# Differential attention and a routed expert layer on one core: projecting queries and keys for eight heads at once, spreading them by DMA, and a new order of the side work

## The chip, the cores and the metric

The kernel runs on one NeuronCore of a Trainium2 chip. Its engines are TensorE (PE, matrix products), VectorE (DVE), ScalarE (ACT), GpSimd (POOL) and SyncE (SP, which here only issues DMAs). Each works through its own queue of instructions in order; semaphores tie the queues together. The metric is the time on the device, in microseconds, of one execution. Three runs of the kernel before gave 842.52, 847.56 and 846.54 us, median 846.54.

## The reference, cut to what matters

The input x is eight sequences of 256 tokens with 256 features, 2048 tokens in all. Two blocks follow each other, each on a layer-normalized copy, each added to x.

```python
q = (x @ wq.T).reshape(b, t, 16, 2, 8);  k = likewise;  v = (x @ wv.T).reshape(b, t, 16, 16)
attn = attn(q1, k1, v) - lambda_full * attn(q2, k2, v)     # softmax over the 256 tokens of a sequence
attn = attn * rsqrt(mean(attn * attn) + eps) * subln_w * (1 - LAMBDA_INIT)
x = x + attn @ wo.T
logits = xn @ gate_w.T                                      # 32 experts
sel = top 4 of logits;  w = softmax over the chosen four
x = x + sum over sel of w * expert(xn) + 0.05 * sum over sel of w * small_expert[sel // 2](xn)
```

There are 16 heads, each with two queries and two keys of 8 features (the two halves of the head) and values of 16 features. The large experts have an inner size of 96, the sixteen small ones of 128; each is silu(gate) times up, then down. All data are 32-bit floats.

## The kernel before, in words

**Tiling.** The 2048 tokens are taken in four iterations (`NIT`) of 512 tokens (`TB`, two sequences). Four heads make a group, so an iteration has four steps and attention has 16 steps, numbered s. A step's K and Q lie with four heads in four blocks of 32 rows: a head has 16 rows of features (8 of each half), one row that takes the maximum of each half, and unused rows.

**Projection (`project`, L319 to L340).** The weights are copied once into padded tiles `wk_pad` and `wq_pad` (L135 to L140) in which every head has 32 columns, 16 of them zero. One product of 128 padded columns with 512 tokens (L327, two halves of the contraction) gives a step's K, another its Q, already in the four blocks. ACT copies Q to `qT`, and K twice to `kb`, once for each half, with the other half's rows cleared and the row that subtracts the maximum set (`half`, L337).

**A slot (`both`, L345).** A step has eight slots i. In each, PE makes scores (sc, L358) for step s and, for a step that lies `AHEAD` = 4 slots on, the products from which the row maxima come (sm, L375). ACT takes the exponential of sc (L385), DVE the maximum of sm (L388). sc and sm share three large PSUM buffers (`big`); one small one (`one`) serves everything else. `join_max` (mt, L399) turns the eight slots' maxima and adds them to Q. In odd slots `values` (pv, L412) multiplies probabilities by values, two slots late; `normalize` (po, L430) turns the result, DVE divides by the sums and POOL adds the two halves of a head (L442).

**Side work.** `prologue(it)` normalizes an iteration's tokens, transposes them (tp_a) and makes values (vps, L303). `epilogue(it)` squares and scales the attention output, transposes it (tp_o), multiplies with wo (L476), adds x, normalizes again (tp_f) and calls `route`: logits (lg, L498), the top four one after another (L511 to L530, six DVE operations for each), a mask, running counts and a product that gives every token its position in the list of each expert (pos, L546). Sixteen indirect DMAs from POOL (L582) scatter token number and weight into the lists in HBM. Both functions are generators that yield "pe" or "any"; `fill` (L598) lets one "any" piece go at every slot and one "pe" piece at slots 1, 5 and 7. The order on PE, ACT and DVE is what the program writes (`manual_schedule`); POOL's and SP's is set by a scheduler. The epilogue of iteration it starts in the third slot of the next iteration's first step; that of iteration 3 has nothing to run beside.

**After attention.** The lists are read back, and 95 tiles of 128 list entries go through the experts: POOL fetches token rows (L751), PE multiplies (gu L785, dn L809 and L813), POOL adds the results to HBM (L820). Weights of the small experts and the down weights of the large ones (`wr_sb`, L670 to L679) are loaded by SP into room that attention held, so after attention. The gate and up weights of the large experts (`wl_sb`, L120) are loaded at the start.

Of the kernel before, what the change touches and what calls it, by code (L numbers as in the profile page):

```python
# [14 lines left out]
MANUAL = {mybir.EngineType.PE, mybir.EngineType.Activation, mybir.EngineType.DVE}  # L15

P = 128
# [21 lines left out]
def kernel(  # L39
# [23 lines left out]
    keep = ctx.enter_context(tc.tile_pool(name="keep", bufs=3))  # L63
# [31 lines left out]
    wraw = p1.tile([P, 2, 2, E], F32)  # L95
    for i, w in enumerate((wk, wq)):
        nc.scalar.dma_start(out=wraw[:, i], in_=w.rearrange("(kc p) o -> p kc o", p=P))
# [3 lines left out]
    w_sb = {}  # L101
    for n, w in (("v", wv), ("o", wo)):
        w_sb[n] = (p1 if n == "v" else const).tile([P, 2, E], F32, name=f"w{n}_sb")
        nc.scalar.dma_start(out=w_sb[n], in_=w.rearrange("(kc p) o -> p kc o", p=P))
# [6 lines left out]
    load_x(1)  # L111
# [21 lines left out]
    wpad = {}  # L133
    for i, n in enumerate(("k", "q")):
        wpad[n] = p1.tile([P, 2, H, 32], F32, name=f"w{n}_pad")  # L135
        nc.gpsimd.memset(wpad[n], 0.0)
        nc.vector.tensor_copy(
            wpad[n][:, :, :, 0 : 2 * D],
            wraw[:, i].rearrange("p kc (h d) -> p kc h d", d=2 * D),
        )  # L140


# [3 lines left out]
    )  # L146

    nlam = const.tile([P, 1], F32)

    def late_constants():  # L150
# [37 lines left out]
        ebase, [[SLOTS, NE]], base=0, channel_multiplier=0, allow_small_or_imprecise_dtypes=True  # L188
# [34 lines left out]
    with actx:  # L223
# [53 lines left out]
        def transpose_rows(src, dst, tag):  # L277
            for kc in range(2):
                yield "pe"
                tp = one(f"tp_{tag}_{kc}")  # L280
                for a in range(NA):
                    nc.tensor.transpose(
                        tp[:, a * P : (a + 1) * P], src[:, a, kc * P : (kc + 1) * P], ident
                    )
                nc.scalar.copy(dst[:, kc, :], tp)
# [3 lines left out]
        def prologue(it):  # L289
            if it and it + 1 < NIT:  # L290
                load_x(it + 1)
            xT = p2.tile([P, 2, TB], F32, tag="xT", name=f"xT_{it}")
            yield from layernorm_T(x_sb[it], xT, f"a{it}")
            vaug = vaugs[it % 2]
            attn = r2.tile([P, NA, H, 2 * D], F32, tag="attn", name=f"attn_{it}")
            st_it[it] = (xT, vaug, attn)
            for a2 in range(NA // 2):
                yield "pe"
                pv = one(f"vps_{it}_{a2}")
                for i in range(2):  # L300
                    a = 2 * a2 + i
                    for kc in range(2):
                        nc.tensor.matmul(  # L303
                            pv[:, i * E : (i + 1) * E],
                            lhsT=xT[:, kc, a * P : (a + 1) * P],
                            rhs=w_sb["v"][:, kc, :],
                            start=(kc == 0),
                            stop=(kc == 1),
                        )
                nc.scalar.copy(  # L310
                    vaug[:, 2 * a2 : 2 * a2 + 2, :, 0 : 2 * D],
                    pv.rearrange("p (a h d) -> p a h d", a=2, d=2 * D),
                )
# [3 lines left out]
        qT, qa, kb, pv, pts = {}, {}, {}, {}, {}  # L317

        def project(s, w):  # L319


            it, g = steps[s]
            cols = slice(g * 4 * 32, (g + 1) * 4 * 32)
            ps = one(f"{w}ps_{s}")
            wv_ = wpad[w].rearrange("p kc h d -> p kc (h d)")
            for kc in range(2):
                nc.tensor.matmul(  # L327
                    ps, lhsT=wv_[:, kc, cols], rhs=st_it[it][0][:, kc, :],
                    start=(kc == 0), stop=(kc == 1),
                )  # L330
            if w == "q":
                qT[s] = p2.tile([P, TB], F32, tag="qT", name=f"qT_{s}", bufs=3)
                nc.scalar.copy(qT[s], ps)
                return
            kb[s] = p2.tile([P, 2, TB], F32, tag="kb", name=f"kb_{s}", bufs=3)
            for h in range(2):
                nc.scalar.activation(  # L337
                    kb[s][:, h, :], ps, AF.Identity,
                    bias=half[:, 1, h : h + 1], scale=half[:, 0, h : h + 1],
                )  # L340
# [66 lines left out]
        def values(s, c):  # L407
# [11 lines left out]
            if c % 2 == 1:  # L419
                oT = p2.tile([P, 512], F32, tag="oT", name=f"oT_{s}_{c}")  # L420
                nc.scalar.copy(oT, pv[s])
                pv[s] = oT

        def normalize(s, bb, oT):
            it, g = steps[s]
            attn = st_it[it][2]
# [6 lines left out]
            pov = po.rearrange("p (r d) -> p r d", d=32)  # L433
            r = p2.tile([P, 16], F32, tag="rsum", name=f"r_{n}")
            nc.vector.reciprocal(r, pov[:, :, 2 * D])
            nc.vector.tensor_scalar(r[:, 8:16], r[:, 8:16], nlam, None, ALU.mult)
            on = p2.tile([P, 16, 2 * D], F32, tag="on", name=f"on_{n}", bufs=3)
# [3 lines left out]
            )  # L441
            nc.gpsimd.tensor_tensor(  # L442
# [6 lines left out]
        def epilogue(it):  # L449
            attn = st_it.pop(it)[2]  # L450
            av = attn.rearrange("p a h d -> p (a h) d")
            yield "any"
            sq = r1.tile([P, NA * H, 2 * D], F32, tag="sq", name=f"sq_{it}")
            nc.gpsimd.tensor_tensor(sq, av, av, ALU.mult)
            yield "any"
# [8 lines left out]
            nc.vector.tensor_tensor(  # L464
                av, av, rms.unsqueeze(2).to_broadcast([P, NA * H, 2 * D]), ALU.mult
            )
            aT = r2.tile([P, 2, TB], F32, tag="eT", name=f"aT_{it}")
            yield from transpose_rows(attn.rearrange("p a h d -> p a (h d)"), aT, f"o{it}")
            xt = x_sb[it]
            for a2 in range(NA // 2):  # L470
                yield "pe"
                ps = one(f"wo_{it}_{a2}")
                for i in range(2):
                    a = 2 * a2 + i
                    for kc in range(2):
                        nc.tensor.matmul(  # L476
                            ps[:, i * E : (i + 1) * E],
                            lhsT=aT[:, kc, a * P : (a + 1) * P],
                            rhs=w_sb["o"][:, kc, :],
                            start=(kc == 0),  # L480
                            stop=(kc == 1),
                        )
                xs = xt[:, 2 * a2 : 2 * a2 + 2, :]
                nc.vector.tensor_tensor(xs, xs, ps.rearrange("p (a e) -> p a e", a=2), ALU.add)
# [6 lines left out]
        def route(it, x2):  # L491
# [16 lines left out]
            chosen = r1.tile([P, TOPK, NA, NE], F32, tag="chosen", name=f"chosen_{it}")  # L508
            top = r2.tile([P, TOPK, NA], F32, tag="top", name=f"top_{it}")
            left = lg  # L510
            for k in range(TOPK):  # L511
                yield "any"
                nc.vector.tensor_reduce(top[:, k], left, AX.X, ALU.max)

                eq = r2.tile(shape, F32, tag="eq", name=f"eq_{it}_{k}")
                nc.vector.tensor_tensor(
                    eq, left, top[:, k].unsqueeze(2).to_broadcast(shape), ALU.is_equal
                )
                nc.vector.tensor_tensor(eq, eq, rev.unsqueeze(1).to_broadcast(shape), ALU.mult)
                mi = r2.tile([P, NA], F32, tag="mi", name=f"mi_{it}_{k}")  # L520
                nc.vector.tensor_reduce(mi, eq, AX.X, ALU.max)
                nc.vector.tensor_tensor(
                    chosen[:, k], eq, mi.unsqueeze(2).to_broadcast(shape), ALU.is_equal
                )
                if k < TOPK - 1:
                    nxt = r2.tile(shape, F32, tag="left", name=f"left_{it}_{k}")
                    nc.vector.scalar_tensor_tensor(
                        nxt, chosen[:, k], -3.0e38, left, ALU.mult, ALU.add
                    )
                    left = nxt  # L530

            yield "any"
            mask = r1.tile(shape, F32, tag="mask", name=f"mask_{it}")
            nc.vector.tensor_reduce(
                mask, chosen.rearrange("p k a e -> p a e k"), AX.X, ALU.add
            )
            yield "any"
            for a in range(NA):
                n = it * NA + a
                nc.vector.tensor_tensor(count[:, n + 1], count[:, n], mask[:, a], ALU.add)  # L540
            yield "pe"
            pos = one(f"pos_{it}")[:, 0 : NA * NE]
            for i, (w, r) in enumerate(
# [12 lines left out]
            entry = r2.tile([P, TOPK, NA, 2], F32, tag="entry", name=f"entry_{it}")  # L556
            wt = entry[:, :, :, 1]
            w4 = [P, TOPK, NA]
            ex = r2.tile(w4, F32, tag="ex", name=f"ex_{it}")
            nc.vector.tensor_tensor(  # L560
                ex, top, top[:, 0].unsqueeze(1).to_broadcast(w4), ALU.subtract
            )
            nc.scalar.activation(ex, ex, AF.Exp)
# [48 lines left out]
        with tc.manual_schedule(engines=MANUAL):  # L612
# [42 lines left out]
            while side:  # L655
                fill()
# [252 lines left out]
```

## Time and profile before

One execution was profiled. It took 878.54 us, of which the span from first to last instruction is 876.8 us; the unprofiled runs have a median of 846.54 us. Times below are from the profiled execution.

| What | us |
|---|---|
| profiled execution, its span | 878.54, 876.8 |
| first maximum product (sm) starts | 24.19 |
| first scores (sc) start | 41.99 |
| Q projections of steps 3 and 12 start | 79.15, 296.88 |
| last transposes of attention (po) start | 448.73 |
| last list scatter is issued, lists are read | 529.68, 533.99 |
| first expert product starts | 543.06 |
| PE busy | 720.9 (82%) |
| DVE, ACT, POOL busy | 374.0 (43%), 322.8 (37%), 339.6 (39%) |

Two things help in reading it. A busy PE is not PE at its peak, since matmuls are pipelined and their ends are modelled. And the share of an engine over the whole span is an average over stages that have different limits, so each stage is read by itself: which instruction waited, and what ended that wait.

### The profile page before, as it was taken

What the parts mean: (1) busy time and instruction counts of PE and PEld (TensorE: products, weight loads), DVE (VectorE), ACT (ScalarE), POOL (GpSimd) and SP (SyncE); (2) the same over time, 40 slices, a digit from 0 to 9 for tenths busy, and PEclk for the clock granted to TensorE, in tenths of its full rate; (3) what the DMA queues carried; (4) which work ended last, traced back from release to release, by engine and by line L of the source; (5) the groups of instructions that cost most, each with busy time, mean ns of one, the idle gap of its engine ahead of it and who ended that gap; (6) DMA issues with size and microseconds to landing.
All of it is one profiled execution on the core that took longest, in us unless ns stands there. A gap on an engine that the chain in (4) does not pass through costs nothing.

```text
span 876.8 us, 11981 instructions
## 1 busy us (share of the span) xinstructions
PE 720.9 (82%) x4201; PEld 429.9 (49%) x4201; DVE 374.0 (43%) x843; ACT 322.8 (37%) x593; POOL 339.6 (39%) x314
## 2 busy tenths in 40 slices
PE   3899999999999869999465302999999999999930
PEld 1334333444444324344244201899777777777720
DVE  1664557655676535776046500233322222222202
ACT  2155445654655333645241100333333333333310
POOL 3000001000010430103410655588888888888850
PEclk9999999999999969999785555999999999999975
DMA  9900000000100000100049801354555455555557
GB/s 267 282 1 1 1 1 1 1 1 26 49 1 1 2 0 4 46 1 2 1 125 237 166 1 44 58 85 81 84 82 83 83 85 85 84 81 84 83 90 253
DMA packets 60300, 58.34 MB, mean 67 GB/s; under 512 B 23122, under 2 KB 56659, under 8 KB 59731
## 3 DMA queue, kind: packets, MB, share of 16 engines
q0 software_dynamic: 20336, 25.12, 17.9%
q1 hardware_dynamic: 36706, 29.32, 12.4%
q10 hardware_dynamic: 3200, 3.15, 1.2%
q8 instruction: 36, 0.59, 0.3%
q14 instruction: 22, 0.17, 0.1%
HBM read 35.73 MB, written 21.82 MB: 66 GB/s over the span
## 4 chain that ended last, share of the span: by engine, by line
PE 68%; DVE 12%; DMA 9%; issue 3%; another core or an unknown queue 3%; POOL 3%; ACT 2%; POOLq 0%; SPq 0%; DVEq 0%; ACTq 0%
PE gu L785 18%; PE sm L375 9%; DVE mp L388 8%; PE sc L358 7%; PE pv L412 6%; PE dn L809 4%; PE dn L813 4%; PE kps L327 4%; PE qps L327 4%; PE xt L759 3%; DMA list_dram<-entry,index 3%; POOL list_dram L582 2%; PE wo L476 2%; DMA y<-sums 2%
## 5 line engine op out<-in xcount | busy, mean ns | idle before, releaser
L388 DVE TENSOR_REDUCE mp<-sm 128x4 f32<-128x1024 f32 x128 | 156.1, 1223 | 145.7 <-PE sm L375 132.1
L385 ACT ACTIVATE pt<-sc 128x1024 f32<-128x1024 f32 x128 | 130.7, 1022 | 144.8 <-PE sm L375 113.7
L820 POOL DMA_INDIRECT sums<-ye,tokens x95 | 151.3, 1593 | 38.7 <-issue 25.0
L358 PE MATMUL sc<-qa,kb 32*128 32x256 f32 x1024 | 163.7, 420 | 2.0 <-issue 1.3
L442 POOL TENSOR_TENSOR attn<-on 128x128 f32<-128x128 f32 x32 | 16.9, 529 | 369.3 <-DVE on L438 354.8
L375 PE MATMUL sm<-kb,qT 32*128 32x512 f32 x512 | 141.1, 650 | 16.6 <-DVE mp L388 9.0
L761 DVE COPY xTe<-xt 128x256 f32<-128x256 f32 x95 | 40.3, 425 | 211.6 <-PE xt L759 199.6
L358 PEld LDWEIGHTS sc<-qa,kb 32*128 32x128 f32 x1024 | 81.8, 187 | 57.0 <-issue 41.9
L751 POOL DMA_INDIRECT xg<-x_dram,tokens x95 | 93.2, 981 | 32.2 <-PE gu L785 13.7
L785 PE MATMUL gu<-wr_sb,xTe 128*128 x380 | 99.3, 384 | 0.0
L785 PE MATMUL gu<-wl_sb,xTe 128*128 x380 | 86.0, 349 | 8.1 <-issue 5.4
L582 POOL DMA_INDIRECT list_dram<-entry,index x64 | 62.2, 972 | 66.4 <-DVE entry L578 39.3
L785 PEld LDWEIGHTS gu<-wl_sb,xTe 128*128 128x128 f32 x380 | 62.2, 192 | 35.9 <-DVE aTe L802 30.2
L785 PEld LDWEIGHTS gu<-wr_sb,xTe 128*128 128x128 f32 x380 | 70.8, 193 | 5.2
L412 PE MATMUL pv<-pt,vaug 128*32 128x512 f32 x512 | 69.9, 619 | 0.1
L794 ACT ACTIVATE act<-gu 128x224 f32<-128x224 f32 x95 | 33.9, 357 | 80.3 <-PE gu L785 70.9
L375 PEld LDWEIGHTS sm<-kb,qT 32*128 32x128 f32 x512 | 37.4, 185 | 47.8 <-DVE mp L388 33.9
L819 ACT ACTIVATE ye<-dn,weights 128x256 f32<-128x256 f32 x95 | 44.8, 472 | 36.8 <-DMA sums<-ye,tokens 32.5
L803 ACT ACTIVATE aTe<-at 128x128 f32<-128x128 f32 x95 | 26.3, 277 | 84.4 <-DVE aTe L802 75.9
L809 PE MATMUL dn<-wr_sb,aTe 96*128 x190 | 56.7, 380 | 0.0
L813 PE MATMUL dn<-wr_sb,aTe 128*128 x190 | 56.6, 379 | 0.0
L759 PE MATMUL xt<-ident,xg 128*128 128x128 f32 x190 | 38.3, 284 | 4.0 <-DMA xg<-x_dram,tokens 3.8
(162 smaller groups left out, 772.0 us busy)
## 6 DMA issues: line engine op xcount, KB each, us to landing
wl_sb<-in_wg_dram SPq DMA_DIRECT2D x4, 768.0 KB, 8.2
wl_sb<-in_wu_dram SPq DMA_DIRECT2D x4, 768.0 KB, 7.4
wr_sb<-in_wd_dram SPq DMA_DIRECT2D x2, 1536.0 KB, 20.8
x<-in_x_dram SPq DMA_DIRECT2D x4, 512.0 KB, 4.2
sums<-zero SPq DMA_DIRECT2D x8, 256.0 KB, 3.2
sums<-x SPq DMA_DIRECT2D x4, 512.0 KB, 2.9
x_dram<-xn_f SPq DMA_DIRECT2D x4, 512.0 KB, 4.4
wr_sb<-in_cwg_dram SPq DMA_DIRECT2D x2, 1024.0 KB, 11.1
```

Source lines behind the costliest of these rows:

```text
L327: nc.tensor.matmul(ps, lhsT=wv_[:, kc, cols], rhs=st_it[it][0][:, kc, :], start=(kc == 0), stop=(kc == 1),)
L358: nc.tensor.matmul(sc[:, j, h * 256 : h * 256 + 256], lhsT=kb[s][rows, h, c * P : (c + 1) * P], rhs=qa[s][rows, qs], start=True, stop=True,)
L375: nc.tensor.matmul(sm[:, j, :], lhsT=qT[m][rows, a * P : (a + 1) * P], rhs=kb[m][rows, :, ks], start=True, stop=True,)
L385: nc.scalar.activation(pt, sc, AF.Exp, scale=SM_SCALE)
L388: nc.vector.tensor_reduce(mps[m % 2][:, a, 2 * mp : 2 * mp + 2, 2 * D : 2 * D + 2], sm.rearrange("p j (s k) -> p j s k", s=2), AX.X, ALU.max,)
L412: nc.tensor.matmul(pv[s][32 * j : 32 * j + 32, :], lhsT=st_it[it][1][:, c, 4 * g + j, :], rhs=pts[(s, c, j // 2)][:, j % 2, :], start=(c % ...
L582: put = nc.gpsimd.indirect_dma_start(list_dram, bass.IndirectOffsetOnAxis(ap=index[:, k, a : a + 1], axis=0), entry[:, k, a], None,)
L751: nc.gpsimd.indirect_dma_start(xg[i], None, x2_dram, bass.IndirectOffsetOnAxis(ap=tokens[:, i : i + 1], axis=0),)
L785: nc.tensor.matmul(ps[:, :, cols], lhsT=xT[i][:, kc, :], rhs=w[:, bass.ds(at + kc * n, n)], start=(kc == 0), stop=(kc == 1),)
L809: nc.tensor.matmul(ps, lhsT=aT[i][0:INTER, 0], rhs=wr[0:INTER, bass.ds(large, E)], start=True, stop=False,)
L813: nc.tensor.matmul(ps, lhsT=aT[i][:, 1], rhs=wr[:, bass.ds(small + (2 * E + 2 * GS), E)], start=False, stop=True,)
L820: nc.gpsimd.indirect_dma_start(sums_dram[i % 2], bass.IndirectOffsetOnAxis(ap=tokens[:, i : i + 1], axis=0), y, None, compute_op=ALU.add, ...
```

## The change: what it does

- K and Q are projected from the unpadded weights: one product gives 128 features, which is eight heads or two steps. It is cut into two parts of 256 tokens. ACT copies the result to a packed tile, and `spread` moves rows by DMA on SP into four standing Q tiles (four DMAs of 16 rows a step) and four standing K tiles (eight DMAs of 8 rows a step). POOL presets these tiles once at the start, so that the rows no DMA writes hold zeros or the row for the maximum.
- SP joins the engines whose order the program writes. All four loads of x are issued at the start, ahead of the gate and expert weights.
- `AHEAD` is 3. Projections sit in slots 0 and 2 of even steps (Q) and 4 and 6 of odd ones (K); po and mt move to slots 3, 5 and 7. Side pieces for PE go into the slots that are left. The pieces are larger: both halves of a transposition, all of vps and all of wo go in one, in a `big` buffer.
- The product with the lambda goes from DVE to POOL, as do the square and the scaling of the epilogue, except in the last iteration.
- The top four come from DVE's operation that returns the eight largest values of a row, with a second one on a key that settles ties, and a third one that finds the four slots. The weights are then picked by comparison.
- A list scatter is a piece of its own ("put"), one for each slot of the program.
- The last epilogue has three `big` buffers to itself.

```diff
-MANUAL = {mybir.EngineType.PE, mybir.EngineType.Activation, mybir.EngineType.DVE}
+MANUAL = {
+    mybir.EngineType.PE, mybir.EngineType.Activation, mybir.EngineType.DVE, mybir.EngineType.SP
+}
...
-    load_x(1)
+    for i in range(1, NIT):
+        load_x(i)
...
+    qTs = [p1.tile([P, TB], F32, name=f"qT{i}") for i in range(4)]
+    kbs = [p1.tile([P, 2, TB], F32, name=f"kb{i}") for i in range(4)]
+    for i in range(4):
+        nc.gpsimd.memset(qTs[i], 0.0)
+        for h in range(2):
+            nc.gpsimd.tensor_copy(
+                kbs[i][:, h, :], half[:, 1, h : h + 1].to_broadcast([P, TB])
+            )
...
         def transpose_rows(src, dst, tag):
+            yield "pe"
+            tp = big(f"tp_{tag}")
             for kc in range(2):
-                yield "pe"
-                tp = one(f"tp_{tag}_{kc}")
...
+        def project(w, p, part):
+            it, gp = p // 2, p % 2
+            if part == 0:
+                packed[w] = p2.tile([P, TB], F32, tag=f"pack{w}", name=f"pack{w}_{p}", bufs=1)
+            ps = one(f"{w}ps_{p}_{part}")[:, 0:256]
+            ts = slice(part * 256, part * 256 + 256)
             for kc in range(2):
                 nc.tensor.matmul(
+                    ps, lhsT=w_sb[w][:, kc, gp * P : (gp + 1) * P],
+                    rhs=st_it[it][0][:, kc, ts], start=(kc == 0), stop=(kc == 1),
                 )
+            nc.scalar.copy(packed[w][:, ts], ps)
+            if part == 1:
+                spread(w, 2 * p)
+
+        def spread(w, s):
+            rows = packed[w][s % 2 * 64 : s % 2 * 64 + 64, :]
             if w == "q":
+                qT[s] = qTs[s % 4]
+                for j in range(4):
+                    nc.sync.dma_start(
+                        out=qT[s][32 * j : 32 * j + 2 * D, :],
+                        in_=rows[2 * D * j : 2 * D * j + 2 * D, :],
+                    )
                 return
+            kb[s] = kbs[s % 4]
+            for j in range(4):
+                for h in range(2):
+                    nc.sync.dma_start(
+                        out=kb[s][32 * j + D * h : 32 * j + D * h + D, h, :],
+                        in_=rows[2 * D * j + D * h : 2 * D * j + D * h + D, :],
+                    )
...
-            nc.vector.tensor_scalar(r[:, 8:16], r[:, 8:16], nlam, None, ALU.mult)
...
+            nc.gpsimd.tensor_scalar(on[:, 8:16, :], on[:, 8:16, :], nlam, None, ALU.mult)
...
+            engine = nc.gpsimd if it + 1 < NIT else nc.vector
+            engine.tensor_tensor(sq, av, av, ALU.mult)
...
+            for a in range(NA):
+                nc.vector.max(top[:, a], lg[:, a])
...
+            for a in range(NA):
+                nc.vector.max(key[:, a], lg[:, a])
...
+            for a in range(NA):
+                nc.vector.max(slot[:, a], slots[:, a])
...
             for k in range(TOPK):
-                yield "any"
                 for a in range(NA):
+                    yield "put"
                     put = nc.gpsimd.indirect_dma_start(
...
-        AHEAD = 4
+        AHEAD = 3
...
+            for w in "kq":
+                for part in range(2):
+                    project(w, 0, part)
+                spread(w, 1)
...
+                if (s + 2) // 2 < NS // 2:
+                    spread("kq"[s % 2], s + 3 - s % 2)
...
+                    kinds = ["pool", "put"]
+                    if i in ((0, 2), (4, 6))[s % 2] and ahead:
+                        project(w, pair, i % 4 // 2)
+                    elif i == 3 and s:
+                        normalize(s - 1, 1)
                         if g == 0:
                             begin(epilogue(it - 1))
+                    elif i == 5 and s + 1 < NS:
                         join_max(s + 1)
+                    elif i == 7:
+                        normalize(s, 0)
+                    else:
+                        kinds.append("pe")
+                    if i not in (3, 7) or it == NIT - 1:
+                        kinds.append("any")
+                    fill(*kinds)
```

## The prediction

> **What bounds the kernel now.** I read first the forty slices and the chain that ended last, both on the page.
>
> ```profile
> PE   3899999999999869999465302999999999999930
> DMA  9900000000100000100049801354555455555557
> PE gu L785 18%; PE sm L375 9%; DVE mp L388 8%; PE sc L358 7%; PE pv L412 6%; PE dn L809 4%; PE dn L813 4%; PE kps L327 4%; PE qps L327 4%; PE xt L759 3%; DMA list_dram<-entry,index 3%; POOL list_dram L582 2%; PE wo L476 2%; DMA y<-sums 2%
> ```
>
> There are four stages: a load stage (DMA at 9, first two slices), attention on PE, a hole in PE (slices 21 to 24) and the experts. The edit leaves the experts alone, so the question is the first three. I then read the timeline at the two ends of attention.
>
> ```profile
> 24.19 1.13 PE L375 MATMUL sm<-kb,qT 32*128 32x512 f32 x4 [0.68 <-ACT qT L333]
> ...
> 36.11 0.72 SPq L215 DMA_DIRECT2D sums<-zero  x1
> 36.87 0.67 SPq L85 DMA_DIRECT2D x<-in_x_dram  x1
> ...
> 41.99 0.70 PE L358 MATMUL sc<-qa,kb 32*128 32x256 f32 x4 [0.60 <-DVE mp L388]
> ```
>
> The first max pass (sm) starts at 24.19 while SP still issues loads and zero fills, until 36.83; before the change attention asks nothing of SP. First scores: 41.99. The last transposes of attention (po) are at 448.73; the first expert product (gu) at 543.06. So: 42 us start, 407 us attention, 94 us tail, 334 us experts and output. Inside attention the timeline shows two consecutive slots:
>
> ```profile
> 181.36 0.70 PE L375 MATMUL sm<-kb,qT 32*128 32x512 f32 x2
> ...
> 182.53 1.23 DVE L388 TENSOR_REDUCE mp<-sm 128x4 f32<-128x1024 f32 x1 [2.77 <-PE sm L375]
> 182.65 1.02 ACT L385 ACTIVATE pt<-sc 128x1024 f32<-128x1024 f32 x1 [0.61 <-PE sm L375]
> ...
> 183.81 0.70 PE L375 MATMUL sm<-kb,qT 32*128 32x512 f32 x2
> ```
>
> With one transpose (po, 0.66) between them, sm to sm is 2.45 us: products, then ACT's exp or DVE's max, then a free buffer. A slot's own scores and sm take 1.1 us of PE. My formula for a slot is max(2.45, 1.1 + filler). The tail, on the chain in order of time:
>
> ```profile
> 493.05 18.58 DMA list_dram<-entry,index
> 529.68 3.50 DMA list_dram<-entry,index
> 533.99 3.10 DMA lists<-list_dram,lrow
> ```
>
> The tail carries iteration 2's routing and all of iteration 3's. The first line is a scatter that took 18.6 us to land beside the expert weight load.
>
> [...] The trace has 2.3 us for the 128 KB fill of x_dram on SP[...]. [...] no row of before shows a small DMA behind large ones. [...] eight vps products of 256 columns and four kps of 512 both take 1.93 us. [...] a 128x1024 square is 1.90 on POOL against 1.22 us for the same shape on DVE.
>
> **The change part by part.**
>
> Start (cost). The spreads are issued by SP in program order, behind the weight loads and the fills. Two more x loads of 512 KB go ahead too; wl_sb issues at 768 KB per 2.4 us give 1.6 us each, so SP reaches the first spread at 36.8 + 3.2 = 40.0. The first sm needs Q of step 0, which is issued after 8 + 8 K pieces: 20 issues at 0.44 us (the start's lone SPq rows are 0.38 to 0.54) = 8.8, and 2.3 to land: 51.1 instead of 24.2. From first sm to first scores before was 17.8 for 12 maxima; now 11 maxima at 1.22 = 13.4, plus vps and the cold clock, say 16: first scores at 67, so **+25** (20 to 32). ACT's copies, POOL's twelve preset operations (about 9 us from 1.2, memsets at 0.51) and the K product are done before 40 and are covered. Step 0 then runs at full clock; before, its K projection took 3.01 instead of 1.98 and 12.8 us passed to the Q projection where the formula gives 10.3: **-2.5**.
>
> Projection (gain). Before, K and Q cost 1.93 each a step. Formula: slot 0 is 1.1 + 1.93 = 3.0, slot 3 with values (1.06) and Q is 4.1, six others 2.45: 21.8. Side pieces, all in slots with values, add six times 0.35 (transposes) and five times 1.65 (vps, wo, lg) and 0.2, a quarter of 10.5 a step: 24.4. The Q projections of steps 3 and 12 of their own count lie at 79.15 and 296.88: 24.2 a step, so the formula holds. After, a pair of steps shares one pass, cut into four half projections (two for K, two for Q), each 2 x 2 instructions of 256 columns at 0.241 = 0.97. Two a step, in slots without values: 1.1 + 0.97 = 2.07, under the 2.45 floor, so hidden. The floor hides them only while slots hold no other filler; uncovered they cost 1.9 a step. po and mt join values in slots 3, 5, 7: 2.8 each. Sum 5 x 2.45 + 3 x 2.8 = 20.65. The side pieces are doubled in size and halved in number: vps and wo at 3.9 add 2.5 each, the two transpose groups that fall into slot 1 add 1.0 each, lg 0.6, pos 0.2: 7.8 / 4 = 1.95. New step 22.6, saving 1.7 over 13 steps = **-23** (-16 to -29). The big pieces take one of three big PSUM buffers; the exp that must free the next one (1.02) ends while the piece runs, so I add nothing; if not, up to 1 us for each of the 15 pieces in the loop (three each of five kinds).
>
> Spreads in the loop. Twelve issues a step at 0.4 (SP's lone stores late in attention are 0.36) are 5 us of SP. The tight one is Q for an even step, issued after slot 2 and read in slot 5: cover is slots 3 and 4 plus the first scores, 2.8 + 2.45 + 0.3 = 5.6 us; need is ACT's exp and copy 0.65, four issues 1.7[...]. So 0, with 1.2 to spare. Each big store SP must issue between (x after wo, xn) waits on DVE or ACT and holds the spreads queued behind it, three times; bound 0 to 4 us each, I take 0. PE's first sm of a step queues behind that wait and, behind it, scores, then ACT's exp. ACT loses 2.0 us a step of evictions and gains 0.8; it is not the bound.
>
> Normalize on POOL and smaller routing. The lambda product moves from DVE (0.23) to POOL (about 0.45); 28 of 32 POOL adds already waited for DVE, covered; in the tail it costs 0.3. Top four: 23 operations of 0.29 become 6 and eight eight-largest, and four more find the slots. No row shows that operation; a 32-wide reduce is 0.18, a 128-wide one 0.29, so 0.15 to 0.3 each; I take 0.18. In attention it is off the path (0). POOL runs a put whenever it reaches it: program order spaces puts, POOL does not wait for slots. Built order puts iteration 0's sixteen in one run still. So "one a slot" itself I cost at 0.
>
> Tail (gain). Iteration 2's epilogue, with fewer slots, reaches its position product just after the last po, so only its sixteen puts (16 x 1.28 = 20) are left and run beside iteration 3. That packs more into steps 14 and 15: +2. Iteration 3 alone from 450.4: POOL 0.9, square, mean, rsqrt, scale with iteration 2's DVE work between 8.5, transposes and copy 3.7, wo at cold clock 7.6, add and statistics 3.7, rsqrt 1.7, normalize and transposes 3.4, copy 1.0, lg 3.9, top four 4.5, positions and slots 5: first put at 494. Then 16 x 1.28 and 3.4 to land: lists at 518 instead of 534.0: **-16** (-10 to -22; from below, if slow landings under the weight load hold POOL's eight-deep rotation as they did between 499 and 512).
>
> Sum: 25 - 2.5 - 23 + 2 - 16 = -14.5. The profiled execution is 878.54 (span 876.8 and 1.7 around it): 864. The median of the runs is 846.54, 32 below; I subtract the same amount there, since the stages changed are timed by engines and DMA issue, not by a share of the whole: **832**.
>
> **Rivals.**
>
> Stalls gone. Both put bursts inside attention are followed by waits for which the profile names no engine:
>
> ```profile
> 316.73 1.22 DVE L388 TENSOR_REDUCE mp<-sm 128x4 f32<-128x1024 f32 x1 [10.14 <-remote]
> 432.15 1.02 ACT L385 ACTIVATE pt<-sc 128x1024 f32<-128x1024 f32 x1 [6.66 <-remote]
> ```
>
> PE loses about 22 us there (20 us windows 300 to 320 and 420 to 440 hold 10.9 and 10.3 of PE). If puts cause them and the new order breaks the bursts, 832 - 22 = 810. For: they end 2 us after the last put. Against: the burst at 481 to 499 stalls nothing, and POOL still issues runs.
>
> Late spreads (slower). [...] It decides when Q's landing passes 3.3 us. At 6 us: 2.75 x 7 even steps = 19, the start's eight-deep rotation makes 0.75 of each 0.44 issue (+6) and landing +4: 832 + 29 = 861. For: constants of 8 to 24 KB took 4.9 to 6.8 us at the loaded start. Against: 2.3 us for 128 KB once the load thinned.
>
> A wash. The floor of 2.45 rises with the new rotation of big buffers (the 15 pieces above) and puts still slow the tail (-10 only, then -6 lost): 832 + 15 x 0.7 + 6 = 848; the start's 25 us are then not paid for.
>
> **Chances.** Forecast 0.50, stalls gone 0.17, wash 0.20, late spreads 0.13. About 1% is what a measurement can tell. Faster (under 838): most of the forecast, 0.43, all of the second, 0.17, a little of the wash, 0.05: 0.65. Slower (over 855): 0.13. Same: 0.22. Range: down to 808 for the stalls, up to 853, which leaves out late spreads and a tail of the first.
>
> **What would show it.** Right: no sm before about 50 us and scores near 67; Q projections of successive pairs 45 us apart; no PE wait for a q or kb DMA after step 1; last po near 450, lists about 69 us after it. Wrong: first scores before 55 (spreads overtake the loads); sm waits named DMA in the loop; steps still 24 us; waits on "remote" gone.

## The result, and the profile after

The changed kernel is slower. The profiled execution took 968.98 us, its span 967.0 us (before: 878.54 and 876.8). Against the kernel before the ratio is 1.138, with a 95% interval of 1.127 to 1.149. The median of all five runs is 978.25 us; three of them ran at a lower granted clock than the other two and are left out of the ratio. The forecast was 832 us, with a range up to 853.

The forty slices of the changed kernel, from its page:

```profile
PE 790.5 (82%) x4201; PEld 498.6 (52%) x4201; DVE 352.1 (36%) x784; ACT 303.9 (31%) x561; POOL 368.1 (38%) x361
...
PE   3079999999989999999999651069999999999950
...
PEclk9575699899999899995557765579999999999985
DMA  9810000010011000440001199425555555554557
```

A slice is 24.2 us. PE is full up to slice 22 (532 us; before up to slice 19 of 21.9 us each, 416 us), and now carries 790.5 us instead of 720.9, although the projections shrank. In slices 4 and 19 to 21 its clock stands at 5 while it is busy at 9. The chain that ended last is no help here, since for this execution it reaches back only to the experts.

The start, from the timeline (start, duration, engine, line, output and inputs, in brackets the idle time before it and what ended it):

```profile
40.00 10.85 SPq L353 DMA_DIRECT2D kb<-packk  x16
50.95 4.97 SPq L345 DMA_DIRECT2D qT<-packq  x8
52.98 2.62 PE L391 MATMUL sm<-kb,qT 32*128 32x512 f32 x4 [30.09 <-DMA qT<-packq]
...
73.34 0.70 PE L374 MATMUL sc<-qa,kb 32*128 32x256 f32 x4 [1.21 <-DVE qa L421]
```

SP reaches the spreads at 40.00, as forecast, and the first sm starts at 52.98 (forecast 51.1). First scores come at 73.34 (forecast 67).

A slot in the middle of attention at full clock, same view:

```profile
214.49 0.70 PE L374 MATMUL sc<-qa,kb 32*128 32x256 f32 x4
...
215.03 1.02 PE L391 MATMUL sm<-kb,qT 32*128 32x512 f32 x4
215.88 0.60 PE L374 MATMUL sc<-qa,kb 32*128 32x256 f32 x4
...
216.41 1.09 PE L288 MATMUL tp_a<-ident,xn_a 128*128 128x128 f32 x8
```

Scores, maximum products, scores: one after another, 1.92 us before PE is free for the next thing. In the kernel before, the same products took 1.07 us, from 181.34 to 182.41:

```profile
181.34 0.48 PE L358 MATMUL sc<-qa,kb 32*128 32x256 f32 x2
...
182.41 0.66 PE L430 MATMUL po<-ident,oT 128*128 128x128 f32 x4
```

The waits say the same from the other side (total us, times, longest): ACT's exp waits 255.8 us for PE where the largest such row of before has 113.7, DVE's maximum 211.9 where it had 132.1.

```profile
ACT pt L401 <- PE sc L374: 255.8, 120, 5.9
DVE mp L404 <- PE sm L391: 211.9, 115, 45.1
...
PE sm L391 <- DMA qT<-packq: 30.1, 1, 30.1
```

The last line is the only wait of PE that this view puts down to a spread, the one at the start.

The tail:

```profile
547.70 0.66 PE L447 MATMUL po<-ident,oT 128*128 128x128 f32 x4 [0.76 <-ACT oT L437]
...
580.65 18.94 SPq L507 DMA_DIRECT2D sums<-x  x1
589.00 1.19 POOL L607 DMA_INDIRECT list_dram<-entry,index  x1 [10.05 <-DMA list_dram<-entry,index]
...
620.12 0.97 POOL L607 DMA_INDIRECT list_dram<-entry,index  x1 [0.30 <-DMA x_dram<-xn_f]
627.80 0.99 POOL L754 DMA_INDIRECT lists<-list_dram,lrow  x1 [6.72 <-issue]
```

From last po to the reading of the lists it is 80.1 us; before it was 85.3. The scatters of iteration 2 and the x store of iteration 3 stand among the weight load's transfers: a scatter waits 10 us for a landing, and the store needs 18.9 us to be issued.

### The profile page after: what moved, and what is told of

Read it like the earlier page. It is cut to its first block, busy times and chain, and to the rows that moved or that the text cites. A ratio compares the mean times of both kernels' runs of the same rounds, so it can differ in the third digit from the quotient of the medians.

```text
span 967.0 us, 12278 instructions
## 1 busy us (share of the span) xinstructions
PE 790.5 (82%) x4201; PEld 498.6 (52%) x4201; DVE 352.1 (36%) x784; ACT 303.9 (31%) x561; POOL 368.1 (38%) x361
## 5 line engine op out<-in xcount | busy, mean ns | idle before, releaser
L404 DVE TENSOR_REDUCE mp<-sm 128x4 f32<-128x1024 f32 x128 | 156.1, 1223 | 214.0 <-PE sm L391 211.9
L401 ACT ACTIVATE pt<-sc 128x1024 f32<-128x1024 f32 x128 | 130.6, 1023 | 259.7 <-PE sc L374 255.8
L391 PE MATMUL sm<-kb,qT 32*128 32x512 f32 x512 | 156.5, 706 | 46.9 <-DMA qT<-packq 30.1
L374 PE MATMUL sc<-qa,kb 32*128 32x256 f32 x1024 | 184.6, 460 | 1.2 <-DVE qa L421 1.2
L458 POOL TENSOR_SCALAR on<-on,nlam 128x128 f32<-128x128 f32 x32 | 19.7, 615 | 409.1 <-DVE on L454 388.3
L374 PEld LDWEIGHTS sc<-qa,kb 32*128 32x128 f32 x1024 | 99.8, 214 | 105.0 <-issue 92.5
L797 DVE COPY xTe<-xt 128x256 f32<-128x256 f32 x95 | 40.3, 424 | 207.4 <-PE xt L795 207.4
L391 PEld LDWEIGHTS sm<-kb,qT 32*128 32x128 f32 x512 | 53.1, 214 | 69.3 <-issue 32.4
L428 PE MATMUL pv<-pt,vaug 128*32 128x512 f32 x512 | 84.5, 739 | 0.0
```

The lines of the kernel that those rows point to most:

```text
L374: nc.tensor.matmul(sc[:, j, h * 256 : h * 256 + 256], lhsT=kb[s][rows, h, c * P : (c + 1) * P], rhs=qa[s][rows, qs], start=True, stop=True,)
L391: nc.tensor.matmul(sm[:, j, :], lhsT=qT[m][rows, a * P : (a + 1) * P], rhs=kb[m][rows, :, ks], start=True, stop=True,)
L401: nc.scalar.activation(pt, sc, AF.Exp, scale=SM_SCALE)
L404: nc.vector.tensor_reduce(mps[m % 2][:, a, 2 * mp : 2 * mp + 2, 2 * D : 2 * D + 2], sm.rearrange("p j (s k) -> p j s k", s=2), AX.X, ALU.max,)
L428: nc.tensor.matmul(pv[s][32 * j : 32 * j + 32, :], lhsT=st_it[it][1][:, c, 4 * g + j, :], rhs=pts[(s, c, j // 2)][:, j % 2, :], start=(c % ...
```

## The experiments

**The theory.** In `both`, the scores of slot i lie in the row block `jp = 1 - i % 2` (64 of the 128 rows of K and Q, two heads of 32), and the maximum products in `mp = k % 2`, where k is i plus the lookahead, modulo 8. With a lookahead of 4, mp is i % 2, the other block. With 3 it is 1 - i % 2, the same block. The two timelines above have the same products in 1.07 us with different blocks and in 1.92 us with the same one. If the block is what decides, the change from 4 to 3 made products that ran side by side run in turn. The rivals: the doubled pieces and the new order cost the time, or the clock does.

**Rows put apart again, all else as changed.**

```diff
-                c, jp = i // 2, 1 - i % 2
+                c, jp = i // 2, i % 2
```

> The changed kernel with one token altered: the scores of slot i use row block i%2 rather than 1 - i%2[...]. Row theory (the lookahead of 3 put both on the same rows, so they run one after the other, 1.9 us a slot rather than 1.06): a slot's products take 1.1 us again, attention from first scores to last po falls from 474 to 384 us (22.6 a step), the profiled span from 967 to about 880, the median to 855 to 885. Rival A (the doubled pieces in three big buffers, and the start's and the puts' order, cost the time): nothing moves by more than 10 us, span 955 to 975. Rival B (cold clock after the long start wait is the cause): the two stretches at half clock stay, span above 930.

Measured: 845.5 us, ratio to the kernel before 0.998 (0.996 to 1.000). The one token is worth some 120 us. A slot of this kernel on the timeline:

```profile
181.46 0.48 PE L374 MATMUL sc<-qa,kb 32*128 32x256 f32 x2 [0.29 <-DVE mp L404]
181.47 0.70 PE L391 MATMUL sm<-kb,qT 32*128 32x512 f32 x2
181.78 0.60 PE L374 MATMUL sc<-qa,kb 32*128 32x256 f32 x4
182.01 0.59 PE L391 MATMUL sm<-kb,qT 32*128 32x512 f32 x2
182.21 0.38 PE L374 MATMUL sc<-qa,kb 32*128 32x256 f32 x2
182.53 1.06 PE L428 MATMUL pv<-pt,vaug 128*32 128x512 f32 x8
```

The sm starts 0.01 us after the sc, and pv 1.07 us after the sc: on different rows the two run side by side. So the run shows that the row block decides; what it is that two products on the same rows cannot share, it does not show. First scores to last po falls from 474.8 to 359.6 us. The median is 10 below my range and this stage 24 below the 384 that I expected, which the second profile of the kernel before, below, explains.

**The same token in the kernel before.** At its lookahead of 4, `jp = i % 2` puts the products on the same rows.

> The kernel before with the same token altered, so that at its lookahead of 4 a slot's scores and maxima product share their rows. Row theory: products of a slot take 1.9 us instead of 1.06; with fillers no longer under the 2.45 floor the step goes from 24.4 to about 28, attention grows by 55 to 110 us (the upper end if the half clock stretches show up here too), span 930 to 990. Rivals A and B: the lookahead and the rows cost nothing, span 865 to 890.

Measured: 896.6 us, ratio 1.058 (1.053 to 1.064). A step, from one addition of the maxima to the next over eight steps, goes from 23.4 (in the repeated profile below) to 27.0 us. The rows theory holds in both kernels, but the size differs: 50 us here and some 120 there. The span, 897.4, misses the range of 930 to 990 and lies above that of the rivals. The range was built on a span of 876.8; the next run shows that 845.0 is the one to start from.

**The kernel before, profiled again.**

> The kernel before, unchanged, profiled once more. If the two waits that ended on no named engine, 22 us of PE, belong to the kernel (the stalls rival): they are there again, span 865 to 880, first scores to last po 400 to 410. If they belong to that one execution: they are gone, span 840 to 850, first scores to last po 370 to 380.

Its run took 846.81 us, with a span of 845.0. From its page, and the row of po (first and last start after the durations):

```profile
PE   3899999999999999999763107999999999999930
```

```profile
L430 PE MATMUL po<-ident,oT x128: 272/273/330, 61.9 to 418.8; 128*128 128x128 f32 x128
```

No wait ends on "remote". First scores are at 40.3, first scores to last po takes 378.5 us instead of 407.1, and the first expert product starts at 513.4. So the stalls of the profile that the prediction read belong to that one execution, not to the kernel. This is also why its 878.54 us lay 32 above the median. The stages below are compared with this profile:

| us | before, again | changed | changed, rows apart |
|---|---|---|---|
| first scores | 40.3 | 73.3 | 73.9 |
| first scores to last po | 378.5 | 474.8 | 359.6 |
| last po to first expert product | 94.6 | 88.7 | 91.3 |
| from there to the end | 331.6 | 330.2 | 331.5 |
| span | 845.0 | 967.0 | 856.3 |

Of the 122 us, 33.0 are the start and 96.3 attention, less 5.9 and 1.4. The 96.3 are 115.2 for the shared rows less 18.9 that the rest of the change wins. Both are likely too small. The profiled execution of the kernel with the rows apart took 858.24 us, 12.7 above the median, and has 31 us at half clock in attention. The kernel of the late loads, below, whose steps outside such stretches are as long to 0.1 us, was profiled at 819.18 us, and its attention takes 348.8 us. With that, the two terms are 126 and 30.

**The lookahead itself, rows as written.**

```diff
-        AHEAD = 3
+        AHEAD = 4
```

> The changed kernel with its lookahead back at 4 and its rows as written, so that a slot's scores and maxima are on different rows for the reason they were before. Row theory: 840 to 856, as with the row token altered; the start costs one more maximum, 1.2 us. The spread of Q for an even step now has one slot less of cover, 3.15 us against 4.4 needed: if my sizes hold, maxima wait up to 1.3 us for it in seven steps, 9 in all. If another effect of the lookahead than its rows made the changed kernel slow: off this range to either side by more than 10.

Measured: 865.5 us, ratio 1.023 (1.019 to 1.027). Most of the loss is gone, so the lookahead is what brought the collision in. It lies 10 above the range, and 20 above the run with the rows token. The waits for Q look small:

```profile
PE sm L391 <- DMA qT<-packq: 30.5, 2, 30.0
```

Beyond the start, this leaves 0.5 us. But one wait of 5.1 us, for which the profile names no releaser ("issue"), is a wait for Q too:

```profile
347.32 0.37 SPq L280 DMA_DIRECT2D x_dram<-xn_f  x1
...
348.49 16.15 SPq L353 DMA_DIRECT2D kb<-packk  x16
...
364.74 4.95 SPq L345 DMA_DIRECT2D qT<-packq  x8
...
366.75 1.79 PE L391 MATMUL sm<-kb,qT 32*128 32x512 f32 x2 [5.10 <-issue]
```

These are the first maxima of step 14. Its K pieces stand in SP's queue behind the store of the normalized rows (512 KB), and its Q behind them: sixteen issues took 16.15 us where 0.63 each makes 10. In step 14 of the changed kernel, where the sixteen take 16.54 us, it is one wait: after the store at 409.14, seven K pieces are issued by 415.3, and the eighth, at 420.88, waits 5.5 us for the store to land (`SPq L353 <- DMA x_dram<-xn_f: 5.5, 1, 5.5`). The maxima start 2.0 us after the first Q piece is issued. They start 2.0 us after it in steps 4, 6, 8, 10 and 12 as well, where PE has scores to make meanwhile. The need of 4.4 us was an estimate, and the landing time in it stood in no row of the kernel before; 2.0 us from issue to use is what was measured. Attention takes 375.9 us, 27 more than with the late loads, and 9 of these are the one step with the long wait (32.6 us against 23.2), in which the clock falls to half. The rest is not taken apart.

**Late loads.** With the rows apart, SP issues step 0's K and Q first, then step 1's. x of iterations 1 to 3, gate and the eight `wl_sb` loads become the list `later`, the fills the list `fills`, and both are issued one at a time inside attention.

```diff
-    for i in range(1, NIT):
-        load_x(i)
+    later = [lambda i=i: load_x(i) for i in range(1, NIT)]
...
                 for part in range(2):
                     project(w, 0, part)
+            for w in "kq":
                 spread(w, 1)
+            later.pop(0)()
...
                     fill(*kinds)
+                    if s % 2 == 0 and i >= 5 or s % 2 == 1 and 1 <= i <= 3:
+                        if s % 2 == 1 and later:
+                            later.pop(0)()
+                        elif s % 2 == 0 and fills:
+                            fills.pop(0)()
```

> As the first, and SP issues the first eight spreads that step 0 needs, then those of step 1, before x of iterations 1 to 3, gate, the expert weights and the fills, which follow one at a time inside attention. If the start's 31 us (first scores at 73.3 rather than 42.0) are SP's queue: first scores at 40 to 50, and the span 23 to 33 below the first run, at 845 to 860. If the loads inside attention hold spreads up, first maxima products wait for DMA in the loop and 5 to 15 of it are lost. If the start is the spreads' own issue and landing: first scores stay at 60 or later, and under 12 us are won.

Measured: 824.9 us, ratio 0.977 (0.972 to 0.982). This is the fastest kernel of the study and beats both. It is 20.6 us under the kernel with the rows apart, a little less than the 23 to 33 expected.

```profile
20.96 5.62 SPq L354 DMA_DIRECT2D kb<-packk  x8
...
26.68 2.45 SPq L346 DMA_DIRECT2D qT<-packq  x4
28.67 2.67 PE L392 MATMUL sm<-kb,qT 32*128 32x512 f32 x4 [4.44 <-DMA qT<-packq]
...
50.17 0.48 PE L375 MATMUL sc<-qa,kb 32*128 32x256 f32 x2 [1.15 <-DVE qa L422]
```

First scores are at 50.2 instead of 73.9: of the start's 33 us, 24 were SP's queue. The other 10 are the twelve issues themselves, at 0.70 and 0.61 us each, and their landing. Attention did not suffer from the loads beside it: the profile has PE waiting 6.5 us for spreads in all, 4.4 of them here.

**Late loads with the shared rows.**

> The kernel of the late loads with the changed kernel's rows put back (scores and maxima of a slot on the same rows). Rows and start as separate terms: late loads take their 20 to 24 us off the changed kernel, 945 to 955, with two stretches of 40 and 90 us at half clock as there. If the half clock follows from the start's 28 us wait on PE: no half clock inside attention, so about 60 to 70 us less than the changed kernel, and 50 (what the rows alone cost the kernel before) to 60 above the late loads: 875 to 890.

The edit is the token put back in the kernel of the late loads: `jp = 1 - i % 2`. Measured: 966.6 us, with executions of 963.2, 969.9, 970.6 and 929.8: all far above the second case, and on both sides of the first. Attention of the first execution, from 51.2 to 544.3 us, in one window (durations of PE, PEld, DVE, ACT and POOL, then mean clock, DMA share, GB/s):

```profile
51.20:544.30 493.10, 475.29 (x2519) 241.13 (x2520) 220.45 (x377) 186.80 (x247) 78.34 (x102) 0.80 0.14 35
```

The mean clock is 0.80, lower than the 0.83 of the changed kernel, and in this execution attention loses what the early start wins, 22 us. The execution of 929.8 us is 27 under the fastest of the changed kernel, 957.2, so that this happens always is not shown. Half clock inside attention does not need PE's 30 us wait at the start: it is 5.0 us here. Even the execution of 929.8 us has a mean clock of 0.866 over its span, where the late loads with the rows apart have 0.902 to 0.917.

**Work added to raise PE's use.** Each half projection is made twice, in the changed kernel and in the one with the rows apart.

```diff
-            for kc in range(2):
+            for kc in (0, 1, 0, 1):
```

> The changed kernel with the matmuls of each half projection made twice (the second pass overwrites the first), 0.97 us more of full-array work in two slots a step, 29 us in all at full clock. The changed kernel spends 125 us of attention at half clock (75 to 115 and 430 to 515) though PE is over 90 percent busy there. [...] with more full-array work the half-clock time falls below 60 us, and the total is no higher than 970 in spite of the added work. If the length of those stretches has nothing to do with how much of the array works: they stay 90 to 160 us, and the total is 990 to 1010.

> Control for the run beside it: the same doubling in the kernel with the row token altered. A projecting slot goes from 2.07 us, under the 2.45 floor, to 3.04: 0.6 us twice a step, 17 us in all over the 845.5 of that kernel, so 855 to 868, if the floor hides half projections as I had it. If they were not hidden: 29 us, 872 to 878. The clock stays full inside attention apart from a few us after gaps.

Measured: 973.2 us (956.9 to 978.4) with shared rows, and 864.0 us with rows apart, ratio 1.019 (1.014 to 1.024). The control went as the formula has it: 18.5 us against 17, at a mean clock of 0.97 over attention. With shared rows, the profiled execution, 975.1 us, has a mean clock of 0.87 over 483.3 us of attention: about 125 us at half clock where the changed kernel has about 160. That is less, but not below 60. The total agrees with neither case at its median; only the fastest execution, 956.9, is under 970. That more work of PE over all 128 rows would lift the clock was my guess; the run does not settle what holds it down.

**The tail.** With the rows apart, the second weight load is moved behind the last epilogue and held until iteration 3's last scatter is issued, by a copy on POOL into its target.

```diff
         for _ in epilogue(NIT - 1):
             pass
+        nc.gpsimd.tensor_copy(wr_sb[:, 0, 2 * E : 2 * E + 1], last_entry[0][:, 3, 3, 1:2])
+        for kc in range(2):
+            for i, w in enumerate((cwg, cwu)):
...
```

> As the first, with the second half of the expert weights held back until iteration 3's last scatter has been issued, so that no scatter lands beside it. If the weight load cost the tail its gain (scatters landing in 11.7 us, SP's store of x taking 18.9 us to issue): last po to lists falls from 80 to 62 to 68 us, the sixteen last scatters from 30 to about 20.5; the experts then wait for weights, so the total says nothing. If not: po to lists stays at 76 to 82.

Measured: last po 428.6, lists read at 497.9, 69.3 us instead of 82.3 and just above the 62 to 68 expected; the one run took 869.6 us. The landing of the list scatters in the changed kernel (minimum, median, maximum):

```profile
DMA to landing us min/median/max: 3.1/11.3/20.6
```

and here, with the end of the last burst:

```profile
490.10 0.97 POOL L608 DMA_INDIRECT list_dram<-entry,index  x1 [0.30 <-issue]
497.86 1.00 POOL L756 DMA_INDIRECT lists<-list_dram,lrow  x1 [6.59 <-DMA list_dram<-entry,index]
```

```profile
DMA to landing us min/median/max: 3.8/7.3/13.2
```

The last sixteen scatters follow each other without a wait for a landing, from 471.0 to 490.1. The weight load is what took the tail's gain; but the experts cannot start without it, and first products with those weights come only at 536.9.

**Half of the load held.** On top of the late loads, only the last three of the seven transfers wait.

```diff
         for _ in epilogue(NIT - 1):
             pass
+        nc.gpsimd.tensor_copy(wr_sb[0:INTER, 0, 0:1], last_entry[0][0:INTER, 3, 3, 1:2])
+        for i in range(2):
+            nc.sync.dma_start(
+                out=wr_sb[0:INTER, :, i * E : (i + 1) * E],
...
```

> The kernel of the late loads with the last three of seven transfers of the second weight load (what the down products need, 3.7 of 8 MB) held until iteration 3's last scatter is issued. If the load's length beside the scatters is what slows them: last po to lists from 76 to 68 to 72 and the total to 816 to 822. If the first half of the load is what matters: no change, or the down products wait for their weights, up to 10 us more.

Measured: 829.3 us, ratio to the kernel before 0.981 (0.977 to 0.985). Lists come at 71.6 us after the last po (76.0 without), as expected; but the first expert product then starts 19.5 us after the lists, instead of 9.2. The gain in the scatters is paid back where the load moved to, and the total misses the 816 to 822.

## Why the prediction was wrong

**The step that failed** is "A slot's own scores and sm take 1.1 us of PE", and its reuse in the sum for the new step. It was read in the kernel before, and it held there only because the two lay on different rows. The lookahead of 3 was in the diff; I followed it through the number of maxima before the first scores and through the cover of the spreads, but not through `mp`. With 1.92 in the same formula a new step is two slots with a half projection (2.89), two at the floor of 2.45, one with values (2.98), three with values and a transpose (3.64), together 24.6, and 1.95 of side pieces: 26.5. The four steps of the changed kernel that follow its first half clock stretch took 26.2, 27.2, 24.9 and 27.4. No rival had this mechanism either: each looked at waits and queues, and this is neither.

**The clock.** The sum assumed full clock in attention, and won 2.5 us from it in step 0. 0.83 over 474.8 us is about 160 us at half clock, 41 of them from 74 us on, where the scores begin. The experiments show that it goes with the shared rows in this kernel (0.83 and 0.80 against 0.96 and 0.99). No run takes it apart from the rows, but the trace allows an estimate. From 189.7 to 270.9 and from 326.9 to 407.1 us the changed kernel makes six steps at a clock of 1.00, each 26.9 us on average; the same six take 22.2 with the rows apart. 4.7 us a step is some 75 over 16 steps for the products in turn, which leaves some 40 of the 115.2 to the half clock. The kernel before with shared rows, at 0.98, agrees: its attention grows by 56 us, from 378.5 to 434.6.

**The start** (+25 forecast, +33.0 measured). The first sm was right to 2 us. The size was off behind it: first sm to first scores took 20.4 us instead of 16, and the repeated profile starts 1.7 earlier than the first. That the queue of SP sets it was right; the late loads took 24 back.

**The projection gain** was right in its mechanism and small in its size. Over the fifteen intervals from one addition of the maxima to the next, a step takes 23.7 us in the repeated profile and 21.8 with the late loads: 1.9 less, where the forecast has 1.7 and both sums are about 0.7 us too long. But it counted 13 steps of the 16. Attention gains 18.9 us with the rows apart, in the execution with 31 us at half clock, and 29.7 with the late loads, where the forecast has 23 less the 2 for steps 14 and 15. The control shows that the floor hides the half projections.

**Spreads, larger pieces, normalize, routing at 0**: right for the spreads of the changed kernel (30.1 us at the start, nothing later), and with an attention gain of 18.9 to 29.7 us there is no room for the loss of the wash. With the rows apart the same Q of step 14 comes 2.3 us late, and 5.1 with a lookahead of 4: the store ahead of the spreads, bounded at 0 to 4 us and taken at 0, can cost its bound and more. Sizes were off where nothing waits: an eight-largest took 0.18 us as forecast, but they overlap, four in 0.47; the product on POOL took 0.62, not 0.45, a spread's issue 0.6 to 0.7, not 0.4. The list of the change has one move wrong: the square of the epilogue ran on POOL before as well (1.89 us), and the change takes it to DVE in the last iteration (1.23 us, so POOL takes 1.5 times as long here); only the scaling goes to POOL, in the other three.

**The tail** (-16 forecast). From last po to lists (counted from the last of its four starts), 85.6 in the repeated profile became 79.7; held apart from the weight load it is 69.3, which is the forecast 16. The bound "if slow landings under the weight load hold POOL's eight-deep rotation" was named (in the kernel before, the scatter issued at 493.05 landed after 18.58 us, and the eighth after it, at 511.90, waited 3.07 us for that), and I should have taken that end: the moved scatters of iteration 2 fall on the load's beginning.

**The rivals.** Stalls gone: the stalls were not the kernel's. Their 22 us were misread, too: the two windows of 20 us lack 19 of PE, and attention of the two profiles of the kernel before differs by 28.6. Late spreads: not in the changed kernel. Where the slots are faster, one step in an execution has its Q late, by up to 5.1 us, and what makes it late is SP's queue behind a store. Wash: right in its number for the kernel with the rows apart, 845.5, for another reason: the start cost 8 more than forecast, of the tail's 16 only 3.3 came (85.6 to 82.3), and attention gave up to 9 more.

## What to carry to other kernels

Where matmuls use part of PE's rows, the row block of each is part of its price (here 1.07 us for a slot's scores and maxima on different rows, 1.92 on the same): write down which products share rows in each slot, and redo that list for any edit of an index, a lookahead or a loop's phase, since nothing in the waits or queues tells of it beforehand. A duration read for a group of products is a property of the pair, not of each. A wait of PE without a named releaser can be one for a DMA (the 5.10 us with the lookahead of 4): look when the queue issued what the instruction reads. And before a stall in a profile is made a rival, see whether that execution's time lies among the other runs.

## What the runs showed that I had not expected

The clock can stay at half while PE is busy. From the windows of the changed kernel (columns as above):

```profile
430.00:515.00 85.00, 82.11 (x314) 38.08 (x313) 32.77 (x64) 21.72 (x26) 25.41 (x28) 0.51 0.02 3
```

82.1 of 85 us busy, at a mean clock of 0.51; two steps took 40.2 and 43.6 us there, against 26.9 at full clock, so the clock's record is borne out by the time. Shared rows alone do not bring it about: the kernel before with shared rows has a mean clock of 0.98 over its attention.

```profile
40.10:474.70 434.60, 429.49 (x2499) 208.08 (x2500) 231.91 (x406) 201.36 (x267) 52.93 (x66) 0.98 0.03 9
```

That kernel projects with 512 columns at a time and twice as much in all; with the projections doubled, the changed one still spent about 125 us of attention at half clock, where it had about 160. What else it takes stays open.
